# Half a projection behind the next batch's first products, earlier loads of h, and list searches over 24 slots, in a four-layer graph network

## The chip, the cores and the metric

The kernel runs on one core of a Trainium2 chip. The metric is the device time of one execution in microseconds (us). A core has five engines with queues of their own: TensorE (PE; its weight loads are shown as PEld), VectorE (DVE), ScalarE (ACT), GpSimd (POOL) and SyncE (SP, which here only issues DMAs). Each engine takes its instructions in the order in which they were put in its queue, and waits for the semaphores of an instruction before it goes on.

## The reference

The input x has 16 batches of 1024 nodes with 256 features, and adj is a sparse 1024 by 1024 matrix (about 16 non-zeros in a row). Four graph layers follow each other. The change lies in the first:

```python
pre_u = jnp.einsum('bud,dk->buk', h_t, W1[:d])
pre_v = jnp.einsum('bvd,dk->bvk', h_t, W1[d:])
hidden = jax.nn.relu(pre_u[:, :, None, :] + pre_v[:, None, :, :] + b1)
S = jax.nn.sigmoid(jnp.einsum('buvk,ko->buvo', hidden, W2)[..., 0] + b2[0])
a_t = jnp.einsum('buv,bud->bvd', S * A_a, h_t)
m_t = jnp.einsum('uv,bud->bvd', A_m, h_t) * h_t
z_t = beta1 * h_t + beta2 * (jnp.einsum('bvd,de->bve', a_t, Wa) + ba) + beta3 * (jnp.einsum('bvd,de->bve', m_t, Wm) + bm)
```

A_a and A_m are both adj. S is needed only where adj is not zero. The other three layers are a layer of neighbour sums with a ReLU and two attention layers; they come after the stage in question.

## The kernel before

Each row of adj has up to 32 non-zeros. A preparation (up to about 100 us) finds their values with VectorE, and loads and turns the first four batches. From then on two streams of work run beside each other, and a generator interleaves them in program order.

The main stream of the stage in question is `score_free` (line 942): all of the first layer that needs no score S. It first turns adj (`turn_adj`), and then goes through the 16 batches. For a batch from the fifth on, `edge_sides` (line 315) makes pre_u, pre_v and h Wa for 8 node tiles, two banks of PSUM a tile, evicted by ScalarE into the tile st (two buffers), from which SP stores them to u_d, v_d and hw_d. `messages` (line 342) makes adj times h in four groups of eight products; VectorE multiplies each with hT into a quarter of mT (line 353). Then the next batch is brought: its h and hT are loaded (`load_kept`, the first four), or its h is loaded (`load_h`) and turned on TensorE by `turned` (line 302), whose four banks are evicted by VectorE and ScalarE in turn (`evacuate`, lines 141 and 143). Last, `without_edges` (line 357) projects mT with Wm, in two halves of four products; VectorE adds beta1 hT (line 368) and SP stores zb. PSUM has eight banks, given out in turn.

The second stream, `score_steps` (line 717), makes the scores for the listed edges, a slot at a time. A slot is one list place of 128 nodes for four batches. GpSimd gathers 128 rows of v_d (`fetch`, line 708), four slots ahead into six buffers. VectorE adds u (line 825) and takes the ReLU and multiplies with W2 (line 827). ScalarE sums over the features (line 831). After the 16 slots of a tile come the sigmoid and the products with adj; they are put on a list, `waiting`, and GpSimd scatters them into a dense array, dense_d (line 713). Node tiles have 16 places of their own; a node with more non-zeros has the rest in extra rows of four places, which other slots work on from slot 128 on.

The places are found by `search` (line 742): `max_index` on a row of adj for eight values. The first 16 places of all eight tiles are searched ahead of slot 0, the other 16 places, two searches a tile, in slots 0 to 7. Then `places` (line 747) works out where they go, and `to_extra_rows` (line 768) packs them and puts 32 scatters into extra_d on the list `moving`; each slot issues one of these after its gather and its dense scatters. Twelve slots after the last of them SP loads the packed rows, and 24 later VectorE unpacks them.

What sets the order: `Side.along` lets the second stream take 0.26 of a slot for each microsecond that the main stream names in its yields (`PACE`, "free"), so the place of the slots among the products is written out by hand. Each slot's add waits for one of the last products (`paced`), so that the slots do not run ahead of TensorE. From slot HOLD = 40 on a slot issues one dense scatter, or two in every odd slot while more than four are waiting. A scatter is put behind the last gather:

```python
for _ in range(0 if n < HOLD else 2 if n % 2 and len(waiting) > 4 else 1):
    if waiting:
        group, *what = waiting.pop(0)
        ins = scatter(*what)
```

In the profile all products have line 131 (`product`), all gathers line 708 and all scatters line 713; they are told apart by the names of their tiles.

Of the kernel before, what the change touches and what calls it, by code (L numbers as in the profile page):

```python
# [19 lines left out]
GB = 4  # L20
# [4 lines left out]
SLOTS = 32  # L25
FIRST = 16
# [6 lines left out]
FAR = 6  # L33
AHEAD = 3
LEAD = 4
TOP = 16.0


# [32 lines left out]
def gnn_stack_kernel(  # L71
# [28 lines left out]
    B, N, D = x.shape  # L100
    NT = N // P
# [21 lines left out]
    def paced(ins, back=6):  # L123


        if recent:
            after(tc, ins, [recent[max(0, len(recent) - back)]], mybir.DependencyClass.Sync, "keeps pace")
        return ins
# [34 lines left out]
    def with_beta2(w):  # L163
        return nc.vector.tensor_scalar(w[:, :, 2, :], w[:, :, 2, :], beta2, None, ALU.mult)
# [177 lines left out]
    def messages(pools, h, hT):  # L342
        mT = node_pairs(pools[1].tile([P, DH * N], F32, tag="wide", name="mT"))
        for dh in range(DH):
            for v in range(NV):
                cols = slice(v * HN, (v + 1) * HN)
                ps = bank()
                for ut in range(NT):
                    product(
                        ps, h[:, ut, dh * P : (dh + 1) * P], adj_sb[:, ut, cols],  # L350
                        start=ut == 0, stop=ut == NT - 1,
                    )
                nc.vector.tensor_tensor(mT[:, dh, cols], ps, hT[:, dh, cols], ALU.mult)
                yield 6.9
        return mT
# [19 lines left out]
    with ExitStack() as stack:  # L375
# [12 lines left out]
        w1 = load_w1(prep1, nc.scalar)  # L388
# [299 lines left out]
    with tc.If(listed > 0) as arm:  # L688
        with ExitStack() as stack:
# [27 lines left out]
            def score_steps(pool):  # L717
# [24 lines left out]
                def search(part, t):  # L742
                    for lo in range(part.start, part.stop, 8):
                        sl = slice(lo, lo + 8)
                        nc.vector.max_index(slot_v[:, t, sl], slot_a[:, t, sl], adj_sb[:, t, :])
# [12 lines left out]
                own, others = slice(0, FIRST), slice(FIRST, SLOTS)  # L758
# [30 lines left out]
                def unpack(got):  # L789
                    paced(nc.vector.tensor_copy(x_node, got[:, :, : 1 + QUAD]))  # L790
                    nc.vector.tensor_copy(x_a, got[:, :, 1 + QUAD : 1 + 2 * QUAD])
                    nc.vector.tensor_copy(x_at, got[:, :, 1 + 2 * QUAD : 1 + 3 * QUAD])

                ending = []

                def done(group):
# [5 lines left out]
                for n, (g, t, k) in enumerate(todo):  # L802
                    if n + LEAD < len(todo):
                        last = fetch(us, zt, *todo[n + LEAD])
# [4 lines that stand above are left out]
                            group.add(ins)  # L809
                            after(tc, ins, [last], later, "behind the gather")  # L810
                            done(group)
                    if moving:
                        group, *what = moving.pop(0)
                        ins = scatter(*what)
                        group.add(ins)
                        after(tc, ins, [last], later, "behind the gather")
                        arrive = n + 12
                    slots, _, at, av = lists(t)
                    z, u = zt.pop((g, t, k)), us[g, t]
                    if k == 0:  # L820
                        ss[t] = small.tile([P, FIRST, GB], F32, tag="s", name="s")
                    s = ss[t]
                    if k == 0 and (g, t) in follows:
                        sources(us, *follows[g, t])
                    paced(nc.vector.tensor_tensor(z, z, u, ALU.add))  # L825
                    zk = z.rearrange("p (c k) -> p c k", k=D)
                    nc.vector.scalar_tensor_tensor(  # L827
                        zk, zk, 0.0, w2r[:, None, :].to_broadcast([P, GB, D]), ALU.max, ALU.mult
                    )
                    for c in range(GB):  # L830
                        nc.scalar.activation(zk[:, c, :], zk[:, c, :], AF.Copy, accum_out=s[:, k, c : c + 1])  # L831
                    if n < NT:
                        search(others, n)
                    if n == NT:
                        places(others)
                    if n == NT + 4:
                        moved = to_extra_rows()
                    if k == slots - 1:
                        sv = s[:, :slots, :].rearrange("p s c -> p (s c)")
                        nc.scalar.activation(sv, sv, AF.Exp, bias=nb2, scale=-1.0)  # L840
                        nc.vector.tensor_scalar(sv, sv, 1.0, None, ALU.add)
                        nc.vector.reciprocal(sv, sv)
                        gt = small.tile([P, FIRST, GB], F32, tag="g", name="gt")
                        nc.vector.tensor_tensor(
                            gt[:, :slots, :], s[:, :slots, :],
                            av[:, :slots].unsqueeze(2).to_broadcast([P, slots, GB]), ALU.mult,
                        )
                        for j in range(slots):
                            waiting.append((put[g], dense[g % BUFS], at[:, j : j + 1], gt[:, j, :]))
                        if t == last_of[g]:  # L850
                            ending.append(g)
                            while waiting and g == NGR - 1:
                                group, *what = waiting.pop(0)
                                group.add(scatter(*what))
                                done(group)
                    if moved and not moving and n == arrive:
                        got = from_extra_rows(moved)
                    if got is not None and n == arrive + 24:
                        unpack(got)
                    yield  # L860
# [68 lines left out]
            with ExitStack() as first:  # L929
                own1 = first.enter_context(tc.tile_pool(name="own1", bufs=1, reuse_waits="tile"))  # L930
                st_pool = first.enter_context(tc.tile_pool(name="st", bufs=2, reuse_waits="tile"))
                side = Side(score_steps(own1))
                pools = (wide_t, wide_z)
                next_up = load_kept(pools, 0)
                wm = load_wm(own1, nc.sync)
                zero = own1.tile([P, ZERO], F32, name="zero")
                nc.gpsimd.memset(zero, 0.0)

                def stage(n):
                    return st_pool.tile([P, 2 * 3 * D], F32, tag="st", name="stage")[:, :n]  # L940

                def score_free():
                    yield from turn_adj(
                        lambda n: wide_z.tile([P, DH * N], F32, tag="wide", name="stage")
                    )
                    h, hT = next_up
                    for b in range(B):
                        if b == 1:
                            nat = load_naturals(stage)
                            w1 = load_w1(own1, nc.sync)  # L950
                        if b == 2:
                            paced(with_beta2(w1))
                        if b >= GB:
                            yield from edge_sides(st_pool, b, w1, hT)
                        if b == B - 1:
                            first_hw.extend(load_hw(i) for i in range(GB - 1))
                            first_gd.extend(load_gd(0, 0, ut) for ut in range(4))
                        mT = yield from messages(pools, h, hT)
                        now = hT

                        if b + 1 < GB:
                            h, hT = load_kept(pools, b + 1)
                        elif b + 1 < B:
                            h = load_h(pools[0], b + 1)
                            hT = turned(pools[0], h)
                            yield 2.4
                        yield from without_edges(pools, b, now, mT, wm)
                        if b == 1:
                            prepare(nat)
                            yield 3  # L970

                def with_zeros(main):
                    for n, us in enumerate(main):
                        if 7 < n < 40 or n > 40 and n % 3 == 0:
                            clear()
                        yield us

                side.along(with_zeros(score_free()))
                assert not zeros
# [574 lines left out]
```

## Time and profile before

| | |
|---|---|
| median of 3 runs | 3149.95 us (3149.47 to 3156.11) |
| profiled execution, its own time | 3150.39 us |
| its span, first to last instruction | 3148.7 us |
| granted TensorE clock, mean | 0.997 |
| score-free stage | about 100 to 951 us of the span |
| searches (line 745) | 32, of 1219 ns each, from 101.0 to 177.7 us |
| scatters of extra rows into extra_d | 32, the first at 195.9 us |
| first dense scatter | 299.6 us |

The page of a profile lists engines with their busy time, and groups of instructions by line and tiles. "Idle before" is the time in which the engine did nothing ahead of an instruction, and the name behind the arrow is what released it. The timeline gives start and length of instructions in order of time; "x4" stands for four in a row. A window gives each engine's busy time in a stretch. Starts are counted from the span's start. An engine that is idle costs nothing as long as it is not what TensorE waits for.

### The profile page before, as it was taken

To read this page: it belongs to the slowest core of one execution; us is meant where nothing else is said; L and a number is where in the kernel's file an instruction comes from. 1 tells how busy PE (TensorE), PEld (TensorE's weight loads), DVE (VectorE), ACT (ScalarE), POOL (GpSimd) and SP (SyncE) were. 2 spreads that over 40 slices of the span, in tenths; PEclk is the share of its full clock that TensorE was granted. 3 is DMA by queue.
4 is the path that set the end of the run, shared out by engine and by line. 5 is a ranking of instruction groups with operands and counts; after the bars stand their busy time and mean duration, and the time that the engine had idled before them with its cause. 6 is when DMAs were issued, how large, how long until landed. Compare 5 with 4: busy or idle time off the path is not lost. (4 is left out here: it accounts for less than half of the span.)

```text
span 3148.7 us, 39014 instructions
## 1 busy us (share of the span) xinstructions
PE 3082.1 (98%) x11954; PEld 2180.0 (69%) x11954; DVE 2355.3 (75%) x3191; ACT 1942.1 (62%) x6512; POOL 1873.8 (60%) x1483
## 2 busy tenths in 40 slices
PE   9999999999999999999999999999999999999999
PEld 5544544545547756888775688888568888858888
DVE  7887767677774688999667899976789982157844
ACT  3245555566667876787886678788667764414242
POOL 1156788676674577777566776766777760076600
PEclk9999999999999999999999999999999999999999
DMA  9998888787889777568877765787765554485500
GB/s 318 330 331 305 272 289 276 254 255 236 258 289 332 228 212 203 156 199 271 272 226 201 218 162 176 258 283 232 220 205 163 170 190 160 132 258 161 161 4 28
DMA packets 288419, 699.95 MB, mean 222 GB/s; under 512 B 46141, under 2 KB 141178, under 8 KB 281034
## 3 DMA queue, kind: packets, MB, share of 16 engines
q0 software_dynamic: 128224, 387.80, 42.2%
q1 hardware_dynamic: 132538, 258.46, 23.7%
q10 hardware_dynamic: 27440, 51.13, 4.4%
q8 instruction: 96, 1.57, 0.2%
q14 instruction: 121, 0.99, 0.1%
HBM read 565.83 MB, written 131.41 MB: 221 GB/s over the span
## 5 line engine op out<-in xcount | busy, mean ns | idle before, releaser
L831 ACT ACTIVATE z<-z 128x256 f32<-128x256 f32 x2432 | 979.1, 406 | 570.0 <-DVE z L827 500.0
L825 DVE TENSOR_TENSOR z<-z,u 128x1024 f32<-128x1024 f32 x608 | 738.5, 1219 | 396.7 <-PE bank L131 250.2
L131 PE MATMUL bank<-feats,m 128*128 128x257 f32 x4096 | 910.5, 380 | 9.1 <-ACT st L1325 4.4
L708 POOL DMA_INDIRECT z<-v_d,slot_v x512 | 660.0, 1289 | 407.2 <-ACT z L831 233.5
L131 PEld LDWEIGHTS bank<-feats,m 128*128 128x128 f32 x4096 | 768.8, 190 | 121.5 <-ACT st L1325 6.1
L713 POOL DMA_INDIRECT dense_d<-gt,slot_at x512 | 668.4, 1306 | 184.0 <-issue 139.9
L827 DVE SCALAR_TENSOR_TENSOR z<-z,w2r 128x1024 f32<-128x1024 f32 x608 | 737.3, 1219 | 9.0
L131 PE MATMUL bank<-gc,hw 128*128 128x256 f32 x2048 | 453.9, 383 | 17.5 <-ACT gc L1129 9.5
L831 ACT ACTIVATION_READ_ACCUMULATOR z<-z 128x1 f32 x2432 | 461.8, 190 | 0.0
L131 PEld LDWEIGHTS bank<-gc,hw 128*128 128x128 f32 x2048 | 387.5, 191 | 83.3 <-ACT gc L1129 18.8
L131 PE MATMUL bank<-adj_sb,h 128*128 128x512 f32 x1024 | 442.4, 592 | 2.4 <-ACT st L333 1.0
L1099 DVE SCALAR_TENSOR_TENSOR m<-rho,tau,adj_sb 128x512 f32<-128x512 f32 x512 | 375.6, 742 | 65.5 <-PE bank L131 55.6
L131 PE MATMUL bank<-adjT_in,y 128*128 128x512 f32 (+1 forms) x960 | 404.1, 581 | 8.9 <-DMA adjT_in<-adjT_d 7.7
L131 PEld LDWEIGHTS bank<-adj_sb,h 128*128 128x128 f32 x1024 | 194.2, 190 | 242.1 <-issue 238.1
L131 PEld LDWEIGHTS bank<-adjT_in,y 128*128 128x128 f32 x960 | 181.9, 191 | 224.6 <-issue 203.2
L131 PE MATMUL bank<-w,hT 128*128 128x512 f32 (+1 forms) x1024 | 335.3, 488 | 0.0
L1129 ACT ACTIVATE gc<-gd 128x1024 f32<-128x1024 f32 x128 | 264.4, 2068 | 98.7 <-PE bank L131 70.5
L131 PEld LDWEIGHTS bank<-w,hT 128*128 128x128 f32 x1024 | 195.0, 191 | 141.8 <-issue 121.3
L131 PE MATMUL bank<-g_wT,z 128*128 128x257 f32 x1024 | 231.1, 380 | 1.2 <-ACT st L1325 1.1
L131 PEld LDWEIGHTS bank<-g_wT,z 128*128 128x128 f32 x1024 | 191.9, 190 | 32.5 <-issue 3.3
L708 POOL DMA_INDIRECT z<-v_d,x_node x96 | 125.0, 1302 | 129.5 <-ACT z L831 86.7
L1152 DVE SCALAR_TENSOR_TENSOR z<-bank,zbias,z 128x256 f32<-128x256 f32 x128 | 54.6, 479 | 110.5 <-PE bank L131 110.4
(169 smaller groups left out, 2386.7 us busy)
## 6 DMA issues: line engine op xcount, KB each, us to landing
gd<-dense_d SPq DMA_DIRECT2D x128, 512.0 KB
dense_d<-zero ACTq DMA_DIRECT2D x64, 512.0 KB
adjT_in<-adjT_d SPq DMA_DIRECT2D x112, 256.0 KB
h<-in_x_dram SPq DMA_DIRECT2D x19, 1024.0 KB
u_d<-st SPq DMA_DIRECT2D x64, 256.0 KB
v_d<-st SPq DMA_DIRECT2D x64, 256.0 KB
hw_d<-st SPq DMA_DIRECT2D x64, 256.0 KB
u<-u_d POOLq DMA_DIRECT2D x32, 512.0 KB
```

Of the source, the lines that this page charges most:

```text
L131: recent.append(nc.tensor.matmul(*args, **kw))
L708: return nc.gpsimd.indirect_dma_start(out=dst, out_offset=None, in_=src[:], in_offset=bass.IndirectOffsetOnAxis(ap=at, axis=0), **how,)
L713: return nc.gpsimd.indirect_dma_start(out=dst[:], out_offset=bass.IndirectOffsetOnAxis(ap=at, axis=0), in_=src, in_offset=None,)
L825: paced(nc.vector.tensor_tensor(z, z, u, ALU.add))
L827: nc.vector.scalar_tensor_tensor(zk, zk, 0.0, w2r[:, None, :].to_broadcast([P, GB, D]), ALU.max, ALU.mult)
L831: nc.scalar.activation(zk[:, c, :], zk[:, c, :], AF.Copy, accum_out=s[:, k, c : c + 1])
L1099: nc.vector.scalar_tensor_tensor(m, r[:, cols], ta[:, kt : kt + 1], ea[:, kt, cols], ALU.max, ALU.mult)
L1129: paced(nc.scalar.activation(gc, gd.rearrange("p n i -> p i n"), AF.Copy), 16)
L1152: nc.vector.scalar_tensor_tensor(z[i][:, eh, cols], acc[i][eh][:, :QN], zbias[:, eh : eh + 1], z[i][:, eh, cols], ALU.add, ALU.add,)
```

## The change

Three things are changed in the text of the kernel. First, in `score_free` the second half of a batch's `without_edges`, with its store of zb, is issued inside the next batch: behind the first two tiles of its `edge_sides`, or, for the first four batches, behind the first group of its `messages`. Second, the next batch's h (and hT, where it was kept) is requested at the start of a batch rather than after its messages. Third, the 16 later searches are issued one at a time in those of the slots 10 to 33 whose number is no multiple of three, and `places` and `to_extra_rows`, which stood at slots 8 and 12, come at slots 34 and 38.

```diff
+SPREAD = range(10, 34)
...
+                searches = [(lo, t) for lo in range(FIRST, SLOTS, 8) for t in range(NT)]
...
-                    if n < NT:
-                        search(others, n)
-                    if n == NT:
+                    if n % 3 and SPREAD.start <= n < SPREAD.stop:
+                        lo, t = searches.pop(0)
+                        search(slice(lo, lo + 8), t)
+                    if n == SPREAD.stop:
+                        assert not searches
                         places(others)
-                    if n == NT + 4:
+                    if n == SPREAD.stop + 4:
                         moved = to_extra_rows()
...
+                    rest = iter(())
                     for b in range(B):
...
+                        after_h = None
+                        if b + 1 < GB:
+                            after_h = load_kept(pools, b + 1)
+                        elif b + 1 < B:
+                            after_h = load_h(pools[0], b + 1), None
+
+                        steps = messages(pools, h, hT)
                         if b >= GB:
-                            yield from edge_sides(st_pool, b, w1, hT)
+                            sides = edge_sides(st_pool, b, w1, hT)
+                            for _ in range(2):
+                                yield next(sides)
+                            yield from rest
+                            yield from sides
+                        else:
+                            yield next(steps)
+                            yield from rest
...
-                        mT = yield from messages(pools, h, hT)
+                        mT = yield from steps
                         now = hT
-
-                        if b + 1 < GB:
-                            h, hT = load_kept(pools, b + 1)
-                        elif b + 1 < B:
-                            h = load_h(pools[0], b + 1)
-                            hT = turned(pools[0], h)
-                            yield 2.4
-                        yield from without_edges(pools, b, now, mT, wm)
+                        if after_h:
+                            h, hT = after_h
+                            if hT is None:
+                                hT = turned(pools[0], h)
+                                yield 2.4
+                        rest = without_edges(pools, b, now, mT, wm)
+                        yield next(rest)
                         if b == 1:
                             prepare(nat)
                             yield 3
+                    yield from rest
```

## The prediction

> **What bounds the kernel now.** I read first the page's table of engines, then the waits of TensorE from 95 to 960 us (the score-free stage, which the change touches), then the timeline there, and last the windows of that stage. Times are microseconds.
>
> The page's first table: TensorE is the bound, with 66.6 us idle in a span of 3148.7.
>
> ```profile
> PE 3082.1 (98%) x11954; PEld 2180.0 (69%) x11954; DVE 2355.3 (75%) x3191; ACT 1942.1 (62%) x6512; POOL 1873.8 (60%) x1483
> ```
>
> The waits of TensorE between 95 and 960 (waiter, releaser: total, times, longest). All that this change can win is in these lines:
>
> ```profile
> PE bank L131 <- DVE mT L353: 11.8, 5, 3.9
> PE bank L131 <- ACT st L333: 1.0, 1, 1.0
> PE bank L131 <- DMA h<-in_x_dram: 0.7, 1, 0.7
> ```
>
> The timeline of TensorE shows where: twice in batch 0, then at the ends of batches 6 and 7. In a row: start, length, then in brackets the idle time before.
>
> ```profile
> 141.47 3.70 PE L131 MATMUL bank<-mT,wm 128*128 128x512 f32 x8 [1.79 <-DVE mT L353]
> 149.06 4.54 PE L131 MATMUL bank<-mT,wm 128*128 128x512 f32 x6 [3.88 <-DVE mT L353]
> ...
> 433.74 2.84 PE L131 MATMUL bank<-mT,wm 128*128 128x512 f32 x6 [2.56 <-DVE mT L353]
> ...
> 493.52 4.54 PE L131 MATMUL bank<-mT,wm 128*128 128x512 f32 x6 [2.80 <-DVE mT L353]
> ```
>
> Batches 6 and 7 wait on VectorE, and VectorE waits on a gather, as its timeline at the end of batch 6 shows:
>
> ```profile
> 429.58 1.23 DVE L825 TENSOR_TENSOR z<-z,u 128x1024 f32<-128x1024 f32 x1 [3.96 <-DMA z<-v_d,slot_v]
> ...
> 430.73 2.35 DVE L827 SCALAR_TENSOR_TENSOR z<-z,w2r 128x1024 f32<-128x1024 f32 x2
> ...
> 433.00 0.68 DVE L353 TENSOR_TENSOR mT<-bank,hT 128x512 f32<-128x512 f32 x1
> ...
> 433.60 1.28 DVE L141 COPY hT<-bank 128x512 f32<-128x512 f32 x2
> ```
>
> The product of that mT was finished at 425; its eviction stood in VectorE's queue behind two slots' work until 433. And the gather is late because GpSimd issues without a pause. Its timeline:
>
> ```profile
> 316.59 1.45 POOL L708 DMA_INDIRECT z<-v_d,slot_v  x1 [0.30 <-issue]
> 318.35 1.50 POOL L713 DMA_INDIRECT dense_d<-gt,slot_at  x1 [0.30 <-issue]
> 320.15 0.97 POOL L713 DMA_INDIRECT dense_d<-gt,slot_at  x1 [0.30 <-issue]
> 321.43 0.97 POOL L713 DMA_INDIRECT extra_d<-xrows,to_u  x1 [0.30 <-issue]
> 322.70 0.97 POOL L708 DMA_INDIRECT z<-v_d,slot_v  x1 [0.30 <-ACT st L334]
> ```
>
> One slot there carries a gather, two dense scatters and one scatter of extra rows. The windows (length, then busy time and count of PE, PEld, DVE, ACT, POOL, then clock, DMA share, GB/s) before the dense scatters begin, and after the extra ones end:
>
> ```profile
> 195.93:298.36 102.43, 101.41 (x265) 48.73 (x264) 77.87 (x82) 54.22 (x236) 69.85 (x55) 1.00 0.95 329
> ...
> 326.54:458.60 132.06, 128.86 (x367) 66.69 (x366) 94.59 (x97) 76.72 (x323) 106.77 (x85) 1.00 0.87 274
> ```
>
> In the second, 33 slots take 132.06, 4.00 a slot. TensorE's own pace is 56.72 a batch (transposes of batch 8 at 546.01, of batch 9 at 602.73) for 15 slots, 3.78 a slot. So from slot 44 or so GpSimd is the slower one, by 0.22 a slot. It is carried by its lead: the gather of slot 44 is issued at 298.36, its add runs at 312.9, 14.5 later; by slot 73 the lead is 6.8 (422.79 to 429.58), which is about what a gather needs to land. Before slot 40 the same engine has room: 55 records in 102.43.
>
> **The change part by part.**
>
> *Searches.* 16 searches (1.22 and a load of 0.08 each, 1.30) leave slots 0 to 7 and go one each to 16 of slots 10 to 33. In batch 0 VectorE ran searches one after another while mT waited; without them both waits go. The third group of products ended at 132, its eviction was at 140.75 behind four of these searches (5.2) and would be about 136, before TensorE asks at 139. Gain: the two holes, taken between the pitch of the matmuls, are 141.47 − 139.52 = 1.95 and 149.06 − 145.01 = 4.05. After the second the granted clock was 0.50 for 3.41 us from 149.20, six records in 4.54 instead of 2.84: 1.70 more. Sum −7.7. In slots 10 to 33 a slot costs VectorE 2.44 + 0.87 (two thirds of a search) + 0.6 (four mT of 0.68 and four zb of 0.74 in nine slots) = 3.9 against a pace of 3.8: some 2.5 late after 24 slots, within what batches 1 to 3 allow (6.9, a group). 0; at most +3.
>
> *The extra scatters move too.* This is the part that the words of the change leave out. The lists that `to_extra_rows` packs are ready after `places`, so it goes from slot 12 to slot 38, and its 32 scatters, one a slot, from slots 13–44 to 39–70. The dense scatters start at slot 40 (HOLD) with 32 waiting, three in two slots, and stay at that rate till about slot 95. Today 27 of the 32 extra scatters run in the free time ahead of slot 40 and 5 beside the dense ones; then 31 slots carry 1 + 1.5 + 1 = 3.5 DMAs. Price of one: 132.06 / 85 = 1.55, of which 0.30 is the gap. The shortest is 0.97 + 0.30 = 1.27. Laying the rows of the two engines over each other from 300 to 520, one that starts under the add of L825 takes 1.46, under L827 1.31, with VectorE idle 0.98; since VectorE will idle more, the price falls: its busy share of 94.59/132.06 = 72% becomes about 55%, the excess over 0.97 from 0.28 to 0.21, and the price 1.48. Then 31 × 3.5 × 1.48 + 2.6 (two loads of u) = 163.2. Today the same stretch, from the gather of slot 44 (298.36) to that of slot 75 (430.64), takes 132.3. Difference +30.9. The lead is used up today over that stretch as well, so none of it is cover; and until slot 95 GpSimd is still at 4.00 against 3.78 and gets nothing back. Bounds: all at the shortest, 31 × 3.5 × 1.27 + 2.6 = 140.4, +8; all at 1.55, +38. I take +30.9, since VectorE's two-input work stays as large, only spread. VectorE's queue has mT, zb and the copies of hT behind these adds, and TensorE waits for all three. SP's one load of the packed rows moves from slot 56 to 82 and VectorE's unpacking from 80 to 106, still ahead of slot 112, where the first gather with them is issued: 0.
>
> The Trainium skill, page "SBUF — State Buffer", section "Who interferes with whom", says that a VectorE instruction with two SBUF inputs and a GpSimd instruction that reads SBUF exclude each other, the later one blocking. The 0.98, 1.31 and 1.46 agree in sign. Taken as a full block, each DMA would find its free price of 1.27 whenever VectorE starves, and the sum would sink towards the +8; I stay with the rows.
>
> *Half a projection later.* Until now mT's last quarter is asked for by the eleventh of the sixteen projection records, and hT of the next batch only after all of them. In batch b ≥ 3 the next edge products now follow half a projection, 3.5 instead of 7.0 after the transposes, and they read hT, whose copies (L141) stand right behind that mT. On time (batches 3, 4, 8, 9, 10, 14) the first copy ends 1.8 to 2.1 after the transposes start and is needed at 5.25: 0. Late ones get worse: the copy ended 6.1 (batch 5), 9.3 (6), 9.8 (7), 7.5 (11), 6.0 (12) after it. In 6 and 7 that is about 1.6 more than the holes of today, put once, as the lead is common: +1.5. Batch 11 goes from 0.76 to 2.3 plus ScalarE's half of the copies, batch 12 from 0 to 1.2: +3.1 together.
>
> *zb's store* now stands on SP between the second edge step and the first stores of st, and waits for VectorE's second half; st has two buffers and ScalarE waits for their stores today (hw_d<-st, 25.6 in 10 waits, only 1.0 of it reaching TensorE). Some 1 us less room a batch: +1, bounds 0 and +6.
>
> *h sooner.* On SP the load stands between the last st stores of a batch and the next zb store, before and after the change; it only fetches one batch further ahead. h is landed in time today except 0.7 once, at the first batch, which isn't touched: 0. It adds no DMA.
>
> **Sum.** −7.7 + 30.9 + 1.5 + 3.1 + 1 = +28.8. The profiled execution took 3150.39 around its span of 3148.7, and the median is 3149.95: 3150.39 + 28.8 = 3179.
>
> The Trainium skill, page "TensorE: Matmul & The Clock Gate", Part 1, gives half clock after an idle window of about 3.4 us. The trace agrees after 3.88 and 2.80 and shows none after 2.56. By the page each new long hole would add 1.7, two of them +3.4; I leave that out, since a TensorE that waits for GpSimd at the next batch's end loses nothing by having come slower.
>
> **Rivals.**
> 1. *The order written for VectorE bends (faster).* If mT and hT stand ahead of late adds in VectorE's queue, the lead of the products is kept and slots just slip. Against it: in the stretch that is already late, mT's last eviction stands behind 44, 59, 74 and 89 adds, 15 a batch without drift, though gathers are late. It decides if four or more adds move behind mT there. Then 3150.39 − 7.7 + 1 = 3144, or 3142 with the holes of batches 6 and 7 halved. 0.11.
> 2. *Half of it*: the order bends by two slots (7.6 of cover) and the price is near the low bound: −7.7 + 8 to 20 gives 3150 to 3163, the lower half within 0.2%. 0.14.
> 3. *GpSimd dearer*: in the five slots that carry 3.5 DMAs today, 17 records take 28.18, 1.66 each. At that price 31 × 3.5 × 1.66 = 180, +48, and the sum 3198. 0.07.
> 4. *Cover kept, split harmful*: only the hT step tells, −7.7 + 4.6 + 6 = 3153; its chance is in number 2.
>
> **How the numbers follow.** My forecast 0.68 (3163 to 3196, from +38 and the +3 and +6 bounds at the top), rival 1 0.11, rival 2 0.14, rival 3 0.07. A measurement tells 0.2%, 6.3 us. Faster than 3143.7: most of rival 1, 0.10. Within: 0.08. Slower: 0.82. Range 3149 to 3196 leaves out rival 1, the lowest of 2 and most of 3, together some 0.2.
>
> **What would show it.** The holes at 141 and 149 gone; extra_d scatters from about 285 to 450 instead of 196 to 325; GpSimd over 5 us a slot there; VectorE waiting for z<-v_d far over the 42.1 us of 298 to 520; TensorE holes of 10 to 20 at the ends of batches 5 and 6, released by VectorE's hT copies (L141). Wrong if GpSimd keeps under 4.2 a slot with 3.5 DMAs, or if TensorE runs through while the adds slip.

## The result, and the profile after

The changed kernel took 3198.09 us (median of 6 runs, 3189.7 to 3209.11) against 3149.71 for the kernel before beside it (3145.05 to 3161.78): a ratio of 1.0143, 95% interval 1.0121 to 1.0165. It is 48.4 us slower; 28.8 were forecast, and the median lies 2 us above the top of the range. Disturbed executions are left out of all ratios here; the only ones with times far off were two of the twelve of the version called e8_best below (6628 and 14168 us).

Times below are microseconds. "The stage" is the score-free stage, measured in one profiled execution of each kernel from its first edge product (with adj) to the first product of the next stage (with gc). It took 839.8 before and 883.9 after: +44.1. All code behind it is the same; there the profiled executions spread from 2180 to 2206 (2197.7 before, 2206.3 after), so the rest of the difference isn't told apart from that spread, and the accounts below are of the stage. Medians in the experiments differ by chip as well (before: 3135 to 3150), so each is set against the kernel before on its own chip.

The first table of the page of the changed kernel; TensorE has 105.5 us idle in a span of 3201.1 (66.6 before), and the same 11954 matmuls took it 13.5 longer:

```profile
PE 3095.6 (97%) x11954; PEld 2185.3 (68%) x11954; DVE 2355.7 (74%) x3191; ACT 1943.9 (61%) x6512; POOL 1871.4 (58%) x1483
```

In the stage alone TensorE's busy time went from 826.4 to 838.1 (+11.7) and its idle time from 13.4 to 45.8 (+32.4). The waits of TensorE from 95 to 1010 (waiter, releaser: total, times, longest):

```profile
PE bank L132 <- DVE mT L354: 31.1, 7, 12.3
PE bank L132 <- DVE hT L142: 13.2, 3, 6.2
...
PE bank L132 <- DVE zb L369: 0.8, 1, 0.8
```

The timeline of TensorE, changed kernel (start, length, in brackets the idle time before), shows the places: once in batch 0, twice each at the ends of batches 5 and 6, then at the ends of batches 7 and 11.

```profile
140.99 2.84 PE L132 MATMUL bank<-mT,wm 128*128 128x512 f32 x6 [1.59 <-DVE mT L354]
...
371.22 5.40 PE L132 MATMUL bank<-mT,wm 128*128 128x512 f32 x6 [6.01 <-DVE mT L354]
...
382.85 7.29 PE L132 MATMUL bank<-w,hT 128*128 128x512 f32 x16 [6.23 <-DVE hT L142]
...
449.90 5.32 PE L132 MATMUL bank<-mT,wm 128*128 128x512 f32 x6 [8.46 <-DVE mT L354]
...
467.51 7.63 PE L132 MATMUL bank<-w,hT 128*128 128x512 f32 x16 [12.30 <-DVE mT L354]
...
530.36 6.93 PE L132 MATMUL bank<-w,hT 128*128 128x512 f32 x16 [2.90 <-DVE hT L142]
...
763.35 8.18 PE L132 MATMUL bank<-w,hT 128*128 128x512 f32 x16 [4.06 <-DVE hT L142]
```

Sixteen products with w and hT take 5.32 at full clock; 7.63, 6.93 and 8.18 are the half clock after the hole. The starts of the transposes give the running account, changed against before: −4.9 at batch 5 (362.4, 367.3), +13.7 at batch 6, +36.8 at batch 7, +37.5 from batch 8 to 11, +43.8 from batch 12 to the end.

GpSimd in the stretch of the extra scatters, its timeline of one slot and the first gather of the next:

```profile
408.62 0.98 POOL L709 DMA_INDIRECT z<-v_d,slot_v  x1 [0.30 <-ACT st L335]
409.90 0.99 POOL L714 DMA_INDIRECT dense_d<-gt,slot_at  x1 [0.30 <-issue]
411.20 1.31 POOL L714 DMA_INDIRECT dense_d<-gt,slot_at  x1 [0.30 <-issue]
412.81 0.97 POOL L714 DMA_INDIRECT extra_d<-xrows,to_u  x1 [0.30 <-issue]
414.08 0.98 POOL L709 DMA_INDIRECT z<-v_d,slot_v  x1 [0.30 <-issue]
```

That slot took 5.46, against a TensorE pace of 3.78. The windows from before the dense scatters, over the stretch from gather 44 to gather 75, and from there to gather 93 (length, then busy time and count of PE, PEld, DVE, ACT, POOL, then clock, DMA share, GB/s):

```profile
190.00:295.10 105.10, 105.10 (x274) 50.45 (x273) 82.99 (x106) 58.45 (x254) 42.49 (x31) 1.00 0.92 325
...
295.10:460.65 165.55, 137.88 (x370) 67.58 (x368) 90.61 (x91) 70.54 (x298) 129.52 (x110) 0.92 0.70 218
...
460.65:541.80 81.15, 70.90 (x187) 35.65 (x188) 57.51 (x62) 42.89 (x178) 59.40 (x47) 0.91 0.71 223
```

The middle row is the forecast's step: 110 GpSimd records in 165.55, 1.50 each, where before the same gathers were 132.3 apart. Of that time 129.52 is busy, 1.18 a record; with the gap of 0.30 that is 1.48 each, so GpSimd had next to no time left over. The last row is one that the forecast didn't have: GpSimd is back near its old rate of DMAs a slot, yet these 18 slots took 81.1, against 71.2 before. VectorE's timeline at the end of batch 6 says why:

```profile
461.52 0.18 DVE L1237 TENSOR_SCALAR to_u<-to_u 128x32 uint32<-128x32 uint32 x1 [11.68 <-DMA extra_d<-xrows,to_u]
461.63 2.36 DVE L827 TENSOR_TENSOR z<-z,u 128x1024 f32<-128x1024 f32 x2
...
466.18 0.68 DVE L354 TENSOR_TENSOR mT<-bank,hT 128x512 f32<-128x512 f32 x1
466.78 1.28 DVE L142 COPY hT<-bank 128x512 f32<-128x512 f32 x2
```

Line 1237 caps the list `to_u` in place, for a later use of it as gather indices. All 32 extra scatters read `to_u`, so the overwrite has to wait for the last of them. VectorE's queue has that 0.18 us instruction far ahead of its use, behind add 72 (before: 47). VectorE stood 11.68 there; then came two late slots, mT's eviction and hT's copies. TensorE waited 12.30 and went on at 467.51, as the first of these copies ended (the profile names mT's eviction just ahead of it). The line was in the waits of VectorE before, at a place where it cost TensorE nothing:

```profile
DVE to_u L1218 <- issue: 6.2, 1, 6.2
```

A second instruction waits for the late scatters. VectorE unpacks the packed rows once SP has loaded them, and its queue has this behind add 83 (before: behind add 57, with no wait):

```profile
513.44 0.18 DVE L792 COPY x_a<-got 128x24 f32<-128x24 f32 x1 [7.53 <-DMA got<-extra_d]
```

From there VectorE ran without a wait up to hT's copies at 529.63, for which TensorE waited 2.90 at 530.36. Before, late gathers cost about as much at the end of this batch (2.80 and a half clock of 1.7), so the running account moves by only 0.7 there.

### The profile page after: what moved, and what is told of

It reads as the page before. It is cut to its first block, busy times and chain, and to the rows that moved or that the text cites. A ratio compares the mean times of both kernels' runs of the same rounds, so it can differ in the third digit from the quotient of the medians.

```text
span 3201.1 us, 39024 instructions
## 1 busy us (share of the span) xinstructions
PE 3095.6 (97%) x11954; PEld 2185.3 (68%) x11954; DVE 2355.7 (74%) x3191; ACT 1943.9 (61%) x6512; POOL 1871.4 (58%) x1483
## 5 line engine op out<-in xcount | busy, mean ns | idle before, releaser
L829 DVE SCALAR_TENSOR_TENSOR z<-z,w2r 128x1024 f32<-128x1024 f32 x608 | 737.3, 1219 | 8.7
L132 PE MATMUL bank<-w,hT 128*128 128x512 f32 (+1 forms) x1024 | 345.7, 497 | 26.3 <-DVE hT L142 13.2
L334 ACT ACTIVATE st<-bank 128x512 f32<-128x512 f32 x128 | 75.4, 589 | 106.7 <-PE bank L132 67.9
```

The lines of the kernel that those rows point to most:

```text
L132: recent.append(nc.tensor.matmul(*args, **kw))
L334: nc.scalar.activation(st[:, c, :2, :], ps.rearrange("p (s k) -> p s k", s=2), AF.Copy)
L829: nc.vector.scalar_tensor_tensor(zk, zk, 0.0, w2r[:, None, :].to_broadcast([P, GB, D]), ALU.max, ALU.mult)
```

## The experiments

Stage lengths are of one profiled execution each, and comparable ones scatter by a few microseconds; the ratios are over all runs.

**e1_split**: the changed kernel with the searches, `places` and `to_extra_rows` put back; the split and the sooner h alone.

```diff
-                searches = [(lo, t) for lo in range(FIRST, SLOTS, 8) for t in range(NT)]
...
-                    if n % 3 and SPREAD.start <= n < SPREAD.stop:
-                        lo, t = searches.pop(0)
-                        search(slice(lo, lo + 8), t)
-                    if n == SPREAD.stop:
-                        assert not searches
+                    if n < NT:
+                        search(others, n)
+                    if n == NT:
                         places(others)
-                    if n == SPREAD.stop + 4:
+                    if n == NT + 4:
                         moved = to_extra_rows()
```

> The changed kernel with its searches, places and extra rows put back to slots 0 to 7, 8 and 12; the half projection behind the next batch and the earlier loads of h stay. Read at the start of the first product of the next stage (951.0 us before, 994.8 changed). Theory A, the extra scatters moved into the stretch of dense scatters are the cause: the second hole of batch 0 and its half clock are gone (-5.8), batches 6, 7, 11 and 12 cost 1.6 + 3.1 more, so the stage ends at 947 to 954 and the total is 3145 to 3156. Rival B, the split itself is the cause (hT's copies behind late adds): the stage ends at 975 or later and the total is 3175 or more.

Measured: stage 847.3 (+7.5, end at 957.8: 4 behind theory A's range, 17 ahead of rival B's), total 3143.97 against 3135.26, ratio 1.0026 [1.0013, 1.0039]. By batch 4 it is 4.8 ahead (transposes 194.7 after the stage's start, against 199.5): batch 0's two holes on mT are gone with the searches in their old place; a wait of 2.41 for h of batch 1 has come up instead, with a half clock of 3.4 from 144.9. So the split takes 12.3 later. Its timeline of VectorE has the capped list in batch 5,

```profile
328.25 0.18 DVE L1234 TENSOR_SCALAR to_u<-to_u 128x32 uint32<-128x32 uint32 x1 [8.69 <-DMA extra_d<-xrows,to_u]
```

and that of TensorE its two costly holes:

```profile
332.69 9.63 PE L132 MATMUL bank<-w,hT 128*128 128x512 f32 x24 [5.88 <-DVE zb L369]
...
726.35 8.19 PE L132 MATMUL bank<-w,hT 128*128 128x512 f32 x16 [4.01 <-DVE hT L142]
```

The second half of a projection now takes its banks in the middle of the next batch's edge products, so a zb that VectorE evicts late holds back those products. From the transposes of batch 4 to those of batch 5 it took 64.5 instead of 56.7, from 11 to 12 64.7 instead of 57.7; 2.4 came back between.

**e2_lists**: the kernel before with the third part alone, whose lines stand in the change's diff; `without_edges` and h as before.

> The kernel before with the third part alone: searches over slots 10 to 33, places at 34, extra rows at 38. Theory A: GpSimd needs over 5 us a slot from slot 40 to 70, TensorE waits 25 to 45 us more for VectorE, the stage ends at 975 to 995 and the total is 3175 to 3195. Rival B: the stage ends at 945 to 955, total about 3147, as only holes of batch 0 go.

Measured: stage 869.6 (+29.8, end at 980.2, in theory A's range), total 3167.41 against 3135.26, ratio 1.0109 [1.0083, 1.0136]. Gather 44 to 75 took 162.2. In batch 0 only 1.6 is won (transposes of batch 3 139.9 after the stage's start, against 141.5): the first hole falls from 1.79 to 0.20, the second stays (3.89), and with it a half clock of 3.4 from 148.0. At the end of batch 6 TensorE's timeline has the same pair of holes without any split:

```profile
448.09 5.53 PE L132 MATMUL bank<-mT,wm 128*128 128x512 f32 x8 [6.85 <-DVE mT L354]
...
465.11 4.69 PE L132 MATMUL bank<-mT,wm 128*128 128x512 f32 x6 [11.49 <-DVE mT L354]
```

Lists 29.8 and split 7.5 make 37.3 of the 44.1; 6.8 are left over.

**e5_extra_late**: the kernel before, with the packing of the extra rows alone moved; the searches stay.

```diff
-                    if n == NT + 4:
+                    if n == 38:
                         moved = to_extra_rows()
```

> The kernel before, with nothing changed but that the extra rows are packed at slot 38 instead of 12; searches, places, projections and loads of h stand as before. Theory A: the move of these 32 scatters alone makes the loss of the lists (29.8 us of stage in the third part alone): the stage takes 866 to 874 from the first product with adj (839.8 before), total 25 to 35 over before. Rival C, VectorE's searches in slots 10 to 33 make part of it: 850 to 860.

Measured: stage 874.8 (+35.0), total 3182.05 against 3148.01, ratio 1.0097 [1.0072, 1.0122]. One line's number makes the whole loss of the third part. TensorE's and GpSimd's instructions come in the same order in e5 and e2, and their stages are 5.2 apart: differences of this size between two profiled executions are not to be read.

**e3_hold71**: the changed kernel, the dense scatters held until the extra ones are out.

```diff
-HOLD = 40
+HOLD = 71
```

> The changed kernel with HOLD = 71: the first dense scatter waits until the extra ones are out, so that no slot carries three kinds of DMAs. Theory A: GpSimd keeps the pace of TensorE (3.8 us a slot) from slot 40 to 70, the holes at the ends of batches 5 and 6 go, the stage ends at 945 to 957, total 3143 to 3158; some wait comes later, since 64 scatters wait at slot 71 and are drained at 2.5 DMAs a slot for longer. Rival B: nothing of the loss goes, 985 or later, since the split and the searches are as in the changed kernel.

Measured: stage 859.7 (+19.9, end at 971.3, behind theory A's range), total 3160.29 against 3135.26, ratio 1.0081 [1.0058, 1.0104]. Windows of this kernel, the stretch of the extra scatters and the later one in which the 64 held dense scatters are drained (columns as above):

```profile
299.10:416.80 117.70, 117.70 (x331) 60.01 (x330) 89.76 (x91) 68.65 (x287) 78.43 (x64) 1.00 0.89 299
...
651.90:785.60 133.70, 119.99 (x321) 59.96 (x320) 82.09 (x95) 66.65 (x271) 101.18 (x85) 0.94 0.77 226
```

With two DMAs a slot TensorE has no idle time over the same 31 slots, and no half clock. VectorE's wait at line 1237 shrank to 1.29 as well. The loss returns at the ends of batches 10 to 12, where 8 that had been won turn into 19.9 behind, with 85 records in 133.70. It is the number of GpSimd DMAs per slot that costs, wherever it stands.

**e4_own_index**: the changed kernel, the capped list in a tile of its own.

```diff
+    to_part = const.tile([P, NF], U32, name="to_part")
...
-                nc.vector.tensor_scalar(to_u, to_u, float(XT * P), None, ALU.min)
+                nc.vector.tensor_scalar(to_part, to_u, float(XT * P), None, ALU.min)
...
-                        gather(z, part_d, to_u[:, at : at + 1])
+                        gather(z, part_d, to_part[:, at : at + 1])
```

> The changed kernel, where the capped copy of to_u, which the last stage reads, is written to a tile of its own instead of over to_u. Written over to_u it stands in VectorE's queue behind 72 adds and waited 11.7 us there for the last extra scatter to land. Theory A with this wait as a second term: the wait goes, and since the gather of slot 73 is issued at 451.7 and lands some 5 later, the adds behind it run about 5.7 sooner: the stage ends at 985 to 990. If that wait alone were the term that was missing: all of 11.7 and the clock behind it, 978 to 983. If it hides behind the gathers: 994.

Measured: stage 875.0 (+35.2, end at 986.0, in the first range), total 3174.31 against 3135.26, ratio 1.0118 [1.0094, 1.0142]. By the stages the overwrite cost the changed kernel 8.9, by the medians, each set against its own chip's kernel before, 9.3; the two ratios overlap. Gather 44 to 75 is as before the edit (166.8), and 75 to 93 falls from 81.1 to 69.6.

**e10_late_own**: e5 with that tile.

> The kernel before with the extra rows at slot 38 (874.8 us of stage in that run), and the capped copy of to_u in a tile of its own. Theory: the loss of the late scatters is GpSimd's time by itself, about 25, and the wait at the copy makes 5 to 9 of the 35; the stage takes 865 to 870. If the copy makes most of the loss, 850 or less.

Measured: stage 867.2 (+27.4), total 3167.02 against 3135.95, ratio 1.0109 [1.0086, 1.0133]. By the stages the overwrite makes 7.6 of e5's 35.0. The other 27.4 come with the late scatters themselves: GpSimd's queue, and a wait of VectorE for the packed rows (9.57 here). The ratios of e5 and e10 overlap and can't confirm a gap of 7.6; that it has the same sign in the three pairs with and without the tile (8.9, 7.6 and, below, 3.9) is what speaks for it, with the wait that is gone.

**e9_split_own**: e1 with that tile, to see whether the split's price was the overwrite's.

> The split in all batches and the sooner loads of h, lists as before (847.3 us of stage in that run), and now the capped copy of to_u in a tile of its own. In that run VectorE waited 8.7 at this copy in batch 5's edge products, zb's eviction stood behind it, and TensorE waited 5.9 for the bank and ran 6.8 at half clock. Theory: this goes, 5.9 and some 1.5 of the clock, and the stage takes 839 to 841; what is left of the split is batch 11 (about +7) against the gain in batch 0. If zb's banks wait for late adds anyway: 845 to 847.

Measured: stage 843.4 (+3.6), total 3139.46 against 3135.95, ratio 1.0019 [1.0007, 1.0032]. Between the two expectations. The zb wait at batch 5 is gone, and a wait on hT's copies at the end of batch 5 has come up; TensorE's waits in the stage:

```profile
PE bank L132 <- DVE hT L142: 10.4, 2, 6.5
```

So the overwrite was about half of the 7.5 (3.9). The rest fits the split's loss of leeway, which this line shows, but 3.6 of one execution isn't clear of the scatter.

**e6_even**: the kernel before, with the dense scatters begun when the extra ones are out, and thinned to four in three slots.

```diff
-HOLD = 40
+HOLD = 45
...
-                    for _ in range(0 if n < HOLD else 2 if n % 2 and len(waiting) > 4 else 1):
+                    for _ in range(0 if n < HOLD else 2 if n % 3 == 0 and len(waiting) > 4 else 1):
```

> The kernel before, with the dense scatters evened out: the first at slot 45, when the extra ones are out, and two a slot in every third slot instead of every second while more than four wait. Theory A: GpSimd then has 2.33 DMAs a slot at 1.55, 3.6 us against TensorE's 3.78, and is nowhere the bound: the holes at the ends of batches 6, 7 and 11 (6.1 and a half clock of 1.7) go, the stage takes 830 to 834 and the total falls by 5 to 10. If a gather is late for another reason (a crowded DMA, the buffers): 838 to 841, total unchanged.

Measured: stage 834.5 (−5.3), total 3139.98 against 3148.01, ratio 0.9979 [0.9963, 0.9995]. The holes of batches 6 and 7 go; batch 0's stay, and so does batch 11's (1.32).

**e7_split4**: the kernel before, with h sooner and the split for batches 0 to 2 alone, where it stands behind `messages` and no copy of hT is due.

```diff
-                            for _ in range(2):
-                                yield next(sides)
-                            yield from rest
                             yield from sides
...
-                        yield next(rest)
+                        if b < GB - 1:
+                            yield next(rest)
+                        else:
+                            yield from rest
```

(shown against the changed kernel; the searches are put back as in e1)

> The kernel before with the half projection behind the next batch's first products in batches 0 to 2 alone, where the next batch starts with messages and no hT has to be evicted first, and the sooner loads of h. Theory: the gain of the split without its price: the second hole of batch 0 and its half clock go, 5.8 less, some of it lost to a wait for h of batch 1, which lands no sooner: stage 834 to 837, total 3 to 6 less. If the split costs in the first batches too, 840 or more.

Measured: stage 835.1 (−4.7), total 3144.88 against 3148.01, ratio 0.9986 [0.9971, 1.0001]. The stage agrees; the whole time can't tell it from no change.

**e8_best**: e6, e7 and the list's own tile together.

> The evened dense scatters and the split of batches 0 to 2 together, and the capped copy of to_u in a tile of its own. Theory A: all three gains add, 3 to 6, 6 to 8, and up to 1 for the copy: the stage takes 826 to 830, the total falls by 10 to 15 against the kernel before. Rival: the gains hide each other, since a VectorE that is early in batch 0 only waits more at the gathers: 832 to 836.

Measured: stage 827.7 (−12.1), total 3138.6 against 3148.01, ratio 0.9964 [0.9948, 0.998]: faster than both kernels, by 0.4% against the one before. The stage is in theory A's range; the total fell by 9.4, short of its 10 to 15. Its window from gather 44 to 75, and TensorE's waits on mT in the stage:

```profile
293.20:409.20 116.00, 116.00 (x328) 59.24 (x327) 86.68 (x90) 68.62 (x288) 86.00 (x74) 1.00 0.90 295
```

```profile
PE bank L132 <- DVE mT L354: 3.7, 5, 1.2
```

74 records are busy for 86.00, 1.16 each; with the gap of 0.30 they need 108.2 of the 116.00, or 3.49 a slot. That is under TensorE's 3.78, so GpSimd has time to spare, and TensorE runs without a hole.

## Why the prediction was right in its kind and short in its size

Set against the stage, by the steps of the sum:

| step | forecast | measured | from |
|---|---|---|---|
| batch 0's holes | −7.7 | −4.6 | batch 4's transposes, from the stage's start |
| extra scatters on slots 39 to 70 | +30.9 | +31.4 | e2: 29.8, and the 1.6 that it won first |
| split, batches 6, 7, 11, 12 | +4.6 | +12.3 | e1: 7.5, and the 4.8 that it won first |
| the two together | 0 | +5.0 | the rest |
| zb's store | +1 | 0 | TensorE's waits on st: 0.5, before 1.5 |
| sum | +28.8 | +44.1 | |

**Searches.** This step failed at its first line, "leave slots 0 to 7". The change moves the 16 later searches in the text, but VectorE's queue has them where they were: all 32 run in the same stretch, before and after (durations in ns, then first and last start).

```profile
L745 DVE FIND_INDEX8 slot_v<-slot_a,adj_sb x32: 1216/1219/1223, 101.1 to 177.7; 128x8 uint32<-128x1024 f32 x32
...
L746 DVE FIND_INDEX8 slot_v<-slot_a,adj_sb x32: 1217/1219/1222, 100.4 to 177.2; 128x8 uint32<-128x1024 f32 x32
```

The four ahead of the eviction at 140.75 are later ones, as the prediction read them (they follow line 751, which reads the whole first list), and the changed kernel has the same four there. So the first hole stays (1.59 at 140.99), and the price of searches in slots 10 to 33 never came up. How long this hole is follows the load of wm, for which VectorE waits ahead of the searches: its first use of wm comes 7.3 after the stage's start before (hole 1.79), 7.1 in the changed kernel (1.59) and 5.7 in e2 (0.20), so the 1.6 that e2 won isn't the lists' doing. What removed the second hole was the split, for which nothing was put down in batches 0 to 2; e1 and e7 show it. The packed rows too were ready at about the same time (the last copy into xrows ended at 195.9 before and at 198.6 in the changed kernel). Of the third part, then, what counted is the place of the extra scatters in GpSimd's queue: their first stands at 294, 95 after the rows were ready.

**Extra scatters.** The mechanism held: 165.6 between the two gathers against 163.2 forecast, 1.50 a DMA against 1.48, `extra_d` from 294 to 459 against 285 to 450, 5.3 a slot against "over 5". VectorE's wait for z<-v_d from 298 to 520 rose from 42.1 only to 56.8, not "far", since part of its wait moved to the overwrite. TensorE's holes at the ends of batches 5 and 6 add up to 12.2 and 20.8 ("10 to 20"), and the second of each pair ended with hT's first copy. The agreement of 31.4 with 30.9 is partly luck: without the overwrite the late scatters cost 27.4 (e10), and the overwrite adds 7.6 (e5). GpSimd also got back something, which the prediction ruled out: in e10 its gathers 75 to 93 took 67.5, before 71.2. The overwrite is what the step left out. It named the 32 scatters as moved and not the instruction that waits for the last of them, though that wait stood in the profile of before. The unpacking it did name, at 0 and behind slot 106; VectorE's queue has it behind add 83, where it waited 7.53.

The Trainium skill, page "SBUF — State Buffer", section "Who interferes with whom", makes the port that VectorE and GpSimd share an exclusive lock. The rows of this stretch agree in sign: the 56 DMAs that began with VectorE idle took 0.98, the 29 that began under an add 1.51, the 21 under L829 1.28. So the price is 1.28, with the gap, whenever VectorE starves ("its free price of 1.27"), and the mean is 1.48 because about half of them began under VectorE's work.

**Split.** The mis-sized term. The +3.1 for hT's copies in batches 11 and 12 was of the right kind; in e1 batch 11 alone cost 7.0 and batch 12 nothing: the hole was 4.01, and the half clock behind it 2.9 more (8.19 instead of 5.32). Batch 5's bank wait wasn't seen: the forecast followed mT and hT, not where zb's banks now stand in the ring.

**Half clock.** Leaving it out was right while GpSimd's queue set the pace: e2 lost 31.4 with half clocks, where its gathers lost 29.9. It was wrong at a hole with no other wait close behind it: 530.36 and 763.35 took 1.6 and 2.9 over 5.32, less the 1.7 at batch 7 of before, +2.8. The 2.3 at 467.51 came ahead of the wait at 530.36, and how much of it counts isn't shown. The Trainium skill, page "TensorE: Matmul & The Clock Gate", Part 1, which ties the drop to an idle window of about 3.4 us, spoke against leaving it out. These rows agree that a hole brings half clock, but not in the length: 2.80 was enough before and 2.90 here, so the prediction's "The trace agrees" holds for 3.88 alone.

**h sooner.** 0, as forecast: TensorE waits once for h, 1.1 against 0.7 before.

**Rivals.** Number 1 is refuted: mT's last eviction stands behind 44, 59, 74 and 89 adds, as before. So is 2, that order being part of it. Number 3's price of 1.66 didn't come, though its total did (3198; its own terms add up to 3196), for other reasons: the overwrite and the split. Number 4 kept cover that e2 shows used up.

What stays open: the 5.0 of the two together isn't divided further, and is no larger than the 5.2 between e2 and e5; no run takes the wait for the packed rows away alone; and the 4.3 by which the medians rose more than the stage can't be told from the spread behind it.

## What to carry to other kernels

A line that is moved in the text need not move in its engine's queue: here 16 searches stayed where they were, the packing behind them came 3 us later, and only GpSimd's scatters went, by 98 us. Look the order up in a profile before a gain is put down for it. When a block of work is moved, list what it issues and also what waits for its last instruction; an in-place overwrite of something that its DMAs read is such a waiter, even where it is 0.18 us long and its result is needed much later. Count the DMAs per slot on a queue against the pace of the engine that bounds the kernel: 2.39 at 1.46 were under 3.78 and cost nothing, 3.5 at 1.48 cost some 30 us, and which list they belong to didn't matter. A product moved into another loop takes banks of that loop's ring, so its eviction has to be on time for the loop's own products.

## What the runs showed of the hardware

Half clock came in lengths of 3.4, 6.8, 10.2 and 13.7 us, steps of 3.41. The six in the changed stage began 2.5 to 4.4 after TensorE fell idle and ended 3.0 to 5.6 after it resumed, so a long hole cost 1.6 to 2.9 more behind it, if TensorE was then the one waited for; that it lasts so far into the resumed work wasn't expected.

In each run all half clocks start on one grid of 3.41 us: the six of the changed stage, at 369.58, 379.82, 444.67, 458.33, 530.01 and 762.11, are 3, 19, 4, 21 and 68 steps apart. This grid, laid over TensorE's records in the eleven stages that have half clocks, shows what decides. At full clock, 38 of the 39 drops follow a step in which TensorE was idle for 1.89 or more, and every step with more than 1.96 idle was followed by a drop (the odd one, in e3, follows 0.88). At half clock, every step with 0.75 or more idle was followed by another half step, and every one with 0.53 or less by full clock. So the place of a hole on the grid counts as well as its length: 1.90 inside one step was enough in e1 (492.24), and 2.56 across two steps wasn't before (433.74).

How long a GpSimd DMA took went by what VectorE did as it began, and not by VectorE's busy share alone: the mean was 1.26 at 72% (before, 326.54 to 458.60), 1.18 at 55% (changed) and 1.16 at 75% (e8, 86.68 of 116.00).
